# The first stage of a four-layer kernel: input load, group norm, shifted copies and diagonal matrices done in another way

## The chip, the cores and the metric

The kernel runs as one program on one core of a Trainium2 chip. A core has five engines that run at the same time: TensorE (PE in the profile, with PEld its weight loads), VectorE (DVE), ScalarE (ACT), GpSimd (POOL) and SyncE (SP, which here only issues DMAs). The metric is the device time of one execution in microseconds (us). Before the change it is 3016.59 us, the median of three runs (3013.81 to 3019.69).

## The reference, cut to what matters

The input `x` is (8, 128, 16, 16): 8 images, 128 channels, 256 pixels, all float32. Four layers follow each other. Only the first one and the beginning of the second matter here. The first is `x = x + adder(groupnorm(x), W)`, where the "adder convolution" takes the distance of each 3x3 patch from each filter:

```python
def _gn(v, G=32, eps=1e-5):          # 32 groups of 4 channels, for each image
    ...
    return ((g - m) / jnp.sqrt(s + eps)).reshape(v.shape)

def adder2d(x, W, stride, padding):  # W: (128, 128, 3, 3), padding 1
    ...
    out = -jnp.abs(W_col[:, :, None] - X_col[None, :, :]).sum(1)
```

So each of 128 filters needs, for 9 taps, |w - x| for all 128 channels and 2048 pixels, summed over channels and taps. The second layer is a Mamba branch with short depthwise convolutions; the kernel does these on TensorE with diagonal matrices. Layers three and four are attention, experts, a Performer and a spectral filter; the change does not touch them.

## The kernel before, in words

Channels lie on the 128 partitions. `adder_layer` (L303) does the first layer. Its main loop (L406 to L432) goes over 128 filters, four groups of `FG` = 32, and for each over 9 taps. One step makes a tile `d` of 128 x 2048 from a shifted copy of the normalised image and one weight per channel: either `max(x, w)` on VectorE (L421; two taps may be joined in one tile, L417) or `|w - x|` on ScalarE (L423). TensorE then sums `d` over the partitions with four matmuls of 512 pixels (`add`, L380); the stationary matrix has one column of ones, and the four pixel blocks go to four different groups of 32 columns of the array. For a tap done with `max` the identity |w - x| = 2 max(w, x) - w - x is used, so the sums of x and of w over these taps are needed once: `px` (L386 to L390) sums the images over such taps with 24 matmuls, and `wsum` (L391 to L400) sums the weights with 6 small ones. All matmuls go through the helper at L279, so the profile gives them one line and the tile name tells them apart. Each float32 matmul is two records in the trace.

Ahead of the loop stands the part that the change touches. SP issues the load of `x` in four pieces of two images (L323), then that of the filter weights (L326) and of later layers' weights (L256). ACT's queue issues the constants `cst` (L250; 1261 columns, with the group matrix and the identity in them), `vecs` (L251) and `rows` (L252). One reduction (L346) sums each image per channel, a matmul with the group matrix gives the means `mu`, L350 subtracts them, eight ScalarE instructions square and sum (L354), a second matmul gives the variances, L358 and L362 the inverse root, and eight VectorE instructions (L364) write the normalised image into a zero-bordered tile `pad`. GpSimd zeroes `pad` (L342), and makes three copies of it, `sh0` to `sh2`, shifted by 0, 1 and 2 columns (L371). GpSimd also builds 30 diagonal matrices for the second layer (`diagonals`, L473), with the identity times one vector of `vecs` each; in GpSimd's order these 30 stand ahead of the three copies.

The order of the instructions of an engine comes from a scheduler by priority, except in stretches under `manual_schedule`, where program order is kept. The tiles `d` for VectorE and ScalarE have four buffers each. Semaphores of DMAs are handed out round robin from eight: a ninth DMA waits, on the engine that issues it, until the first of the eight has landed. `mamba_layer` (L453) starts with `first_unit` (L670), which multiplies spare matrices on TensorE in its pauses (`meanwhile`, L676).

Of the kernel before, what the change touches and what calls it, by code (L numbers as in the profile page):

```python
# [54 lines left out]
LN_EXP = "natural_log_exp_and_others"  # L55
GELU = "gelu_and_others"
# [28 lines left out]
def _constants():  # L85

    p = np.arange(P)
    c = {}
    c["ident"] = np.eye(P, dtype=np.float32)
    c["group"] = (p[:, None] // 4 == p[None, :] // 4).astype(np.float32) / 1024.0  # L90
# [78 lines left out]
def _weights(x):  # L169
# [3 lines left out]
    w["adder"] = x["L0_conv_W"].reshape(P, P, 9).transpose(1, 2, 0)  # L173
    w["in_proj"] = x["L1_conv_in_proj_w"].T
# [40 lines left out]
class Env:  # L215
# [32 lines left out]
    def load_shared(self):  # L248
        nc = self.nc
        nc.scalar.dma_start(self.cst, self.dram["cst"])  # L250
        nc.scalar.dma_start(self.vecs, self.dram["vecs"])  # L251
        nc.scalar.dma_start(self.rows, self.dram["rows"].partition_broadcast(P))  # L252

    def load_weights(self):
        for k, t in self.w.items():
            self.nc.sync.dma_start(t, self.dram[k])  # L256

# [42 lines left out]
JOINED = (0, 2)  # L300


def adder_layer(E):  # L303
# [8 lines left out]
    with ExitStack() as ctx:  # L312
# [9 lines left out]
        for b in range(0, B, 2):  # L322
            nc.sync.dma_start(x[:, b : b + 2, :], E.dram["x"][b : b + 2].rearrange("b c s -> c b s"))  # L323
        E.load_shared()
        w = p.tile([P, 9, P], F32, tag="w", name="w0")
        nc.sync.dma_start(w, E.dram["adder"])  # L326
        E.load_weights()
# [13 lines left out]
        pad = p.tile([P, B, 18, 18], F32, tag="pad", name="pad0")  # L341
        nc.gpsimd.memset(pad, 0.0)  # L342


        s1 = p.tile([P, B], F32, tag="s1", name="s1")
        nc.vector.tensor_reduce(s1, x, AX.X, ALU.add)  # L346
        mu = ps.tile([P, B], F32, tag="st", name="mu0")
        E.mm(mu, E.c("group"), s1)
        xc = p.tile([P, B, L], F32, tag="xc", name="xc0")
        nc.vector.tensor_tensor(xc, x, bc(mu[:, :], 2, L), ALU.subtract)  # L350
        s2 = p.tile([P, B], F32, tag="s2", name="s2")
        for b in range(B):
            sq = accp.tile([P, L], F32, tag="sq", name="sq0")
            nc.scalar.activation(sq, xc[:, b, :], AF.Square, accum_out=s2[:, b : b + 1])  # L354
        var = ps.tile([P, B], F32, tag="st", name="var0")
        E.mm(var, E.c("group"), s2)
        rs = p.tile([P, B], F32, tag="rs", name="rs0")
        nc.scalar.activation(rs, var, AF.Sqrt, bias=E.eps)  # L358

        nc.scalar.activation(E.sg, E.r("sigma"), AF.Sqrt)  # L360
        nc.scalar.activation(E.sg, E.sg, AF.Sqrt)
        nc.vector.reciprocal(rs, rs)  # L362
        for b in range(B):
            nc.vector.tensor_scalar_mul(  # L364
                pad[:, b, 1:17, 1:17], xc[:, b, :].rearrange("p (h w) -> p h w", w=16), rs[:, b : b + 1]
            )

        shifted = []
        for kw in range(3):
            t = p.tile([P, B, 18 * 16], F32, tag=f"sh{kw}", name=f"sh{kw}")  # L370
            nc.gpsimd.tensor_copy(t.rearrange("p b (h w) -> p b h w", w=16), pad[:, :, :, kw : kw + 16])  # L371
            shifted.append(t)
        nc.gpsimd.tensor_sub(E.center, E.c("ident"), E.mean)
        diagonals(E)

        def tap(k):
            kh, kw = divmod(k, 3)
            return shifted[kw][:, :, kh * 16 : kh * 16 + L]

        def add(out, lhsT, src, start, stop):  # L380

            for i in range(NBLK):
                E.mm(out[i * FG : (i + 1) * FG, :], lhsT, src[:, 2 * i : 2 * i + 2, :], start, stop)


        px = ps.tile([P, BLK], F32, tag="px", name="px0")  # L386
        for k in MAX_TAPS + MORE_TAPS:
            add(px, neg[:, int(k in MORE_TAPS), :], tap(k), k == MAX_TAPS[0], k == MORE_TAPS[-1])
# [1500 lines left out]
```

## Time and profile before

| what | value |
|---|---|
| median of 3 runs | 3016.59 us (3013.81 to 3019.69) |
| the profiled execution: its time | 3019.29 us |
| the profiled execution: its span, first to last instruction | 3017.5 us |
| PE busy over the span | 2848.3 us, 94% |
| DVE busy | 2426.0 us, 80% |
| ACT busy | 2270.8 us, 75% |
| POOL busy | 724.3 us, 24% |
| mean granted TensorE clock | 0.987 |
| first-layer sums `o` on PE: 8512 records | 922.8 us busy |
| `d` on ACT (L423): 472 | 899.6 us busy |
| `d` on DVE (L421): 592, and joined (L417): 88 | 724.3 and 206.7 us busy |

How to read it: the span is counted from the first instruction of the profiled execution, and all places in time below are counted from there. A row of groups gives the line, engine and operation, the tiles with their shapes, the count, then the busy time and the mean of one instruction in ns, then the idle time of the engine just before, and what ended it. In a table of windows each row is a stretch of time with each engine's busy time and instruction count, then the granted clock (PEclk), the share of the DMA engines, and GB/s. Matmuls overlap, so the mean of one (593 ns) is far longer than the spacing of two.

### The profile page before, as it was taken

How to read it: one execution, taken by the hardware profiler on the slowest of the kernel's cores; microseconds unless marked ns; L12 is line 12 of the kernel's file. 1: busy time of each engine (PE TensorE's matmuls, PEld its weight loads, DVE VectorE, ACT ScalarE, POOL GpSimd, SP SyncE). 2: the span in 40 equal slices, each digit the busy share in tenths (PEclk: the TensorE clock that was granted, in tenths of full speed). 3: DMA queues.
4: the chain of work that ended last, by engine and by line, in shares of the span. 5: the costliest groups of instructions: out<-in, count | busy, mean ns of one | idle time of the engine just before them, and what ended most of it. 6: DMA issues, size and time to landing. Idle time of an engine off the chain costs nothing.

```text
span 3017.5 us, 41743 instructions
## 1 busy us (share of the span) xinstructions
PE 2848.3 (94%) x16356; PEld 1263.0 (42%) x16356; DVE 2426.0 (80%) x3387; ACT 2270.8 (75%) x2739; POOL 724.3 (24%) x441
## 2 busy tenths in 40 slices
PE   6999999999999788998898998999999999999999
PEld 2222222222223233443343454455555555654444
DVE  6999999999998899999899648887777777784210
ACT  5999999999997777777777434577778778777332
POOL 4000000000000699998999400000000000000110
PEclk9999999999999999999999999999999999999999
DMA  1000000000000444444444200000000000001100
GB/s 41 1 2 5 2 1 5 1 1 5 1 1 4 170 144 148 139 144 145 129 153 142 91 22 8 14 1 14 14 14 1 14 14 1 14 1 46 49 28 14
DMA packets 39194, 131.49 MB, mean 44 GB/s; under 512 B 7490, under 2 KB 10572, under 8 KB 37588
## 3 DMA queue, kind: packets, MB, share of 16 engines
q1 hardware_dynamic: 38564, 128.02, 12.4%
q8 instruction: 129, 2.11, 0.3%
q10 hardware_dynamic: 432, 0.79, 0.1%
q14 instruction: 69, 0.57, 0.1%
HBM read 125.91 MB, written 1.84 MB: 42 GB/s over the span
## 4 chain that ended last, share of the span: by engine, by line
PE 70%; DVE 15%; ACT 8%; POOL 3%; issue 2%; DMA 0%; DVEq 0%; ACTq 0%; POOLq 0%
PE o L279 30%; PE p L279 10%; PE acc L279 5%; DVE st L878 5%; PE g L279 4%; PE conv L279 3%; PE pc L279 2%; PE var L279 2%; PE pf L279 2%; PE pconv L279 2%; PE pq L279 2%; POOL dbu L783 1%; ACT da L796 1%; PE pn L279 1%; PE pa L279 1%
## 5 line engine op out<-in xcount | busy, mean ns | idle before, releaser
L279 PE MATMUL o<-d,sel 128*32 128x512 f32 x8512 | 922.8, 593 | 7.5 <-DVE d L421 5.5
L423 ACT ACTIVATE d<-sh,w 128x2048 f32<-128x2048 f32 x472 | 899.6, 1994 | 30.7 <-PE o L279 23.2
L421 DVE TENSOR_SCALAR d<-sh,w 128x2048 f32<-128x2048 f32 x592 | 724.3, 1291 | 14.1 <-PE o L279 10.1
L783 POOL TENSOR_TENSOR dbu<-du,bs 128x1024 f32<-128x1024 f32 x191 | 445.8, 2358 | 969.7 <-DVE du L755 964.2
L279 PEld LDWEIGHTS o<-d,sel 128*32 128x32 f32 x8512 | 273.8, 110 | 655.7 <-issue 533.1
L878 DVE TENSOR_TENSOR_SCAN st<-da,dbu 128x512 f32<-128x512 f32 x384 | 446.3, 1207 | 18.0 <-POOL dbu L783 14.0
L279 PE MATMUL acc<-st,cst 128*128 128x512 f32 x768 | 378.6, 625 | 51.1 <-DVE st L889 50.8
L796 ACT ACTIVATE da<-delta,neg_a 128x510 f32<-128x510 f32 x384 | 256.8, 684 | 78.6 <-DVE st L878 73.3
L279 PEld LDWEIGHTS acc<-st,cst 128*128 128x128 f32 x768 | 146.0, 198 | 252.4 <-issue 145.6
L889 DVE TENSOR_TENSOR st<-st,pcs 128x1024 f32<-128x1024 f32 x168 | 205.2, 1222 | 18.2 <-DVE st L878 0.5
L417 DVE SCALAR_TENSOR_TENSOR d<-sh,w,d 128x2048 f32<-128x2048 f32 x88 | 206.7, 2349 | 1.9
L1824 ACT COPY ug<-p 128x512 f32<-128x512 f32 x128 | 75.0, 586 | 136.6 <-PE p L279 136.6
L1365 POOL TENSOR_TENSOR lw<-lw,turn 128x640 f32<-128x640 f32 x8 | 10.0, 1255 | 685.7 <-DVE turn L1364 592.7
L1142 ACT ACT_TABLE_LOAD x134 | 171.9, 1283 | 2.4
L788 ACT COPY pcs<-cs 128x512 f32<-128x512 f32 x168 | 97.8, 582 | 53.6 <-DVE st L889 49.0
L279 PE MATMUL conv<-pad,f 128*128 128x512 f32 x288 | 135.0, 596 | 0.9 <-ACT pad L1040 0.6
L279 PE MATMUL p<-un,lw 128*128 128x512 f32 x256 | 123.6, 605 | 3.8 <-DVE un L1436 2.1
L279 PE MATMUL p<-g,lw 128*128 128x512 f32 x256 | 116.4, 597 | 3.9 <-ACT g L1150 3.9
L279 PE MATMUL p<-T,H 128*128 128x512 f32 x256 | 113.0, 600 | 0.8 <-DVE H L1753 0.8
L279 PE MATMUL g<-ug,me 128*128 128x512 f32 (+1 forms) x320 | 112.0, 509 | 0.0
L1150 ACT ACTIVATE ex<-ex 128x352 f32<-128x352 f32 x128 | 62.4, 494 | 51.5 <-DVE ex L1633 50.3
L279 PE MATMUL pf<-lw,rk 128*128 128x352 f32 x256 | 97.5, 478 | 0.4 <-DVE ek L1583 0.2
(362 smaller groups left out, 3898.1 us busy)
## 6 DMA issues: line engine op xcount, KB each, us to landing
bs<-rows SPq DMA_DIRECT2D x96, 512.0 KB, 3.8
cs<-rows SPq DMA_DIRECT2D x96, 512.0 KB, 4.7
m<-in_Mphi SPq DMA_DIRECT2D x8, 1024.0 KB, 4.8
lw<-in_layers SPq DMA_DIRECT2D x8, 948.0 KB, 4.6
f<-in_fuse SPq DMA_DIRECT2D x2, 1152.0 KB, 7.8
T<-in_T SPq DMA_DIRECT2D x1, 2064.0 KB, 7.6
x<-in_x SPq DMA_DIRECT2D x4, 256.0 KB, 6.9
total<-sums SPq DMA_DIRECT2D x16, 64.0 KB, 2.0
```

Source lines behind the costliest of these rows:

```text
L279: self.nc.tensor.matmul(out, lhsT=lhsT, rhs=rhs, start=start, stop=stop)
L417: nc.vector.scalar_tensor_tensor(d, tap(k), wk, d, ALU.max, ALU.add)
L421: nc.vector.tensor_scalar(d, tap(k), wk, None, ALU.max)
L423: nc.scalar.activation(d, tap(k), AF.Abs, scale=-1.0, bias=wk)
L783: nc.gpsimd.tensor_tensor(dbs[r], got[r // NST]["du"], bc(row("bs", r), 1, 2), ALU.mult)
L788: nc.scalar.copy(pcs[r], row("cs", r))
L796: nc.scalar.activation(das[g % 3][:, :, 1:], d[:, :, 1:], AF.Exp, scale=a)
L878: nc.vector.tensor_tensor_scan(st[:, h, :], da, dbs[r][:, h, :], 0.0, ALU.mult, ALU.add)
L889: nc.vector.tensor_tensor(st, st, bc(pcs[r][:, :], 1, 2), ALU.mult)
L1142: S.tc.keep_in_program_order(S.nc.scalar.preload_act_table_set(name))
L1150: S.nc.scalar.activation(out, src, func, **kw)
L1824: nc.scalar.copy(dst, p4)
```

## The change

It changes only what stands ahead of the loop over filters, the order of the nine taps of the very first filter, and the place of a few small instructions that it delays into the loop.

- Loads: the group matrix becomes the first 128 columns of `cst` (divided by -1024 now, so that means come out negated) and is loaded by itself, first on ACT's queue. The four pieces of `x` alternate between SP's and ACT's queues. The rest of `cst`, `vecs` and `rows` come after `x`.
- Norm: done in four pairs of images. A reduction of a pair on VectorE, a matmul for its mean, a small copy on ScalarE, two squares on ScalarE with the negated mean as bias; then for each pair a reduction of the squares on VectorE, a matmul, a square root on ScalarE; then for each pair a reciprocal and two `tensor_scalar` that write straight into `sh1`. `sh0` and `sh2` are copied from `sh1` by ScalarE (six pairs) and VectorE (two pairs). GpSimd only zeroes borders.
- Diagonal matrices: 1.97 MB (128 x 3840 float32) made by the host, loaded by SP after all other weights. GpSimd's 30 instructions go.
- Spare products: `meanwhile` multiplies a matrix of ones by itself (128 columns) 6 times at the start, and once or twice after each of the eight small matmuls.
- `px`: 24 matmuls as before, over the same six taps in another order, now all ahead of the first `o`, with the six `wsum` products between the first ones. All of this is in a stretch with the order written by hand.
- `xsum`, `wsum_sb`, `wall` and two square roots of `sigma` move into the loop, to filter 1.

In the built program, the instructions of every engine behind the first filter stand in the same order as before. The order ahead of it, as built, has three waits to note: on ACT's queue `vecs` waits until the group matrix has landed and `rows` until the second pair of `x` has (semaphores handed out again), and the load of the square-root table and all of ScalarE's work stand behind these two; on PE `mu` and `var` share two PSUM buffers, so the third `mu` waits until ScalarE has read the first; and all `o` stand behind the last `px`.

```diff
--- before.py
+++ after.py
@@ -53,6 +53,7 @@
 LN_EXP = "natural_log_exp_and_others"
+SQRT = "sqrt_and_others"
 GELU = "gelu_and_others"
@@ -86,8 +87,9 @@
     p = np.arange(P)
     c = {}
+    c["group"] = (p[:, None] // 4 == p[None, :] // 4).astype(np.float32) / -1024.0
     c["ident"] = np.eye(P, dtype=np.float32)
-    c["group"] = (p[:, None] // 4 == p[None, :] // 4).astype(np.float32) / 1024.0
     sel = np.zeros((P, 2, 4, NH), np.float32)
     for n in range(2):
@@ -171,6 +173,13 @@
     x = {k: np.asarray(a) for k, a in x.items()}
     w["x"] = x["x"].reshape(B, P, L)
     w["adder"] = x["L0_conv_W"].reshape(P, P, 9).transpose(1, 2, 0)
+    diag = np.zeros((P, len(BRANCHES), 2, 5, P), np.float32)
+    p = np.arange(P)
+    for i, s in enumerate(BRANCHES):
+        diag[p, i, :, 0:4, p] = x[f"L1_conv_conv_w_{s}"].reshape(2, P, 4).transpose(1, 0, 2)
+        diag[p, i, :, 4, p] = x[f"L1_conv_D_{s}"].reshape(2, P).T
+    w["diag"] = diag
     w["in_proj"] = x["L1_conv_in_proj_w"].T
     w["xproj"] = np.stack([x[f"L1_conv_xproj_w_{s}"].T.reshape(2, P, NPROJ).transpose(1, 0, 2) for s in BRANCHES], 1)
     w["dtproj"] = np.stack([x[f"L1_conv_dtproj_w_{s}"].T for s in BRANCHES], 1)
@@ -247,13 +256,14 @@
     def load_shared(self):
         nc = self.nc
-        nc.scalar.dma_start(self.cst, self.dram["cst"])
+        nc.scalar.dma_start(self.cst[:, P:], self.dram["cst"][:, P:])
         nc.scalar.dma_start(self.vecs, self.dram["vecs"])
         nc.scalar.dma_start(self.rows, self.dram["rows"].partition_broadcast(P))
     def load_weights(self):
         for k, t in self.w.items():
             self.nc.sync.dma_start(t, self.dram[k])
+        self.nc.sync.dma_start(self.diag, self.dram["diag"])
     def c(self, name):
         a, b = self.cols["cst"][name]
@@ -298,6 +308,50 @@
 MORE_TAPS = (7,)
 MORE = tuple(r for r in range(FG) if r % 10 in (0, 3, 6))
 JOINED = (0, 2)
+PX_TAPS = (4, 7, 0, 6, 2, 8)
+FIRST = (4, 7, 1, 0, 6, 3, 2, 8, 5)
+def start(E, pool, psum, x, shifted):
+    nc = E.nc
+    spare = psum.tile([P, P], F32, tag="px", name="spare")
+    def meanwhile(n):
+        for _ in range(n):
+            E.mm(spare, E.ones, E.ones)
+    def small(name):
+        return pool.tile([P, B], F32, tag=name, name=name)
+    s1, neg_mu, s2, rs = (small(n) for n in ("s1", "neg_mu", "s2", "rs"))
+    sq = pool.tile([P, B, L], F32, tag="sq", name="sq0")
+    pairs = [slice(2 * i, 2 * i + 2) for i in range(NBLK)]
+    meanwhile(6)
+    for b in pairs:
+        nc.vector.tensor_reduce(s1[:, b], x[:, b, :], AX.X, ALU.add)
+        mu = psum.tile([P, 2], F32, tag="st", name="mu0")
+        E.mm(mu, E.c("group"), s1[:, b])
+        meanwhile(2 if b is not pairs[-1] else 1)
+        nc.scalar.copy(neg_mu[:, b], mu)
+        for i in range(b.start, b.stop):
+            nc.scalar.activation(sq[:, i, :], x[:, i, :], AF.Square, bias=neg_mu[:, i : i + 1])
+    for b in pairs:
+        nc.vector.tensor_reduce(s2[:, b], sq[:, b, :], AX.X, ALU.add)
+        var = psum.tile([P, 2], F32, tag="st", name="var0")
+        E.mm(var, E.c("group"), s2[:, b])
+        meanwhile(1 if b is not pairs[-1] else 2)
+        nc.scalar.activation(rs[:, b], var, AF.Sqrt, bias=E.eps, scale=-1.0)
+    for b in pairs:
+        nc.vector.reciprocal(rs[:, b], rs[:, b])
+        for i in range(b.start, b.stop):
+            dst = shifted[1][:, i, 1:17, :].rearrange("p h w -> p (h w)")
+            nc.vector.tensor_scalar(dst, x[:, i, :], neg_mu[:, i : i + 1], rs[:, i : i + 1], ALU.add, ALU.mult)
+        nc.scalar.copy(shifted[0][:, b, 1:17, 1:16], shifted[1][:, b, 1:17, 0:15])
+    for i, b in enumerate(pairs):
+        op = nc.vector.tensor_copy if i < 2 else nc.scalar.copy
+        op(shifted[2][:, b, 1:17, 0:15], shifted[1][:, b, 1:17, 1:16])
 def adder_layer(E):
@@ -319,11 +373,13 @@
         ps = ctx.enter_context(tc.tile_pool(name="l0ps", bufs=2, space=PSUM))
         x = last.tile([P, B, L], F32, tag="x", name="x0")
-        for b in range(0, B, 2):
-            nc.sync.dma_start(x[:, b : b + 2, :], E.dram["x"][b : b + 2].rearrange("b c s -> c b s"))
-        E.load_shared()
+        nc.scalar.dma_start(E.cst[:, :P], E.dram["cst"][:, :P])
+        for i in range(NBLK):
+            two = slice(2 * i, 2 * i + 2)
+            (nc.scalar if i % 2 else nc.sync).dma_start(x[:, two, :], E.dram["x"][two].rearrange("b c s -> c b s"))
         w = p.tile([P, 9, P], F32, tag="w", name="w0")
         nc.sync.dma_start(w, E.dram["adder"])
+        E.load_shared()
         E.load_weights()
@@ -338,66 +394,37 @@
         nc.gpsimd.memset(neg[:, 1, :], 0.0)
         for r in MORE:
             nc.gpsimd.memset(neg[:, 1, r : r + 1], -1.0)
-        pad = p.tile([P, B, 18, 18], F32, tag="pad", name="pad0")
-        nc.gpsimd.memset(pad, 0.0)
-        s1 = p.tile([P, B], F32, tag="s1", name="s1")
-        nc.vector.tensor_reduce(s1, x, AX.X, ALU.add)
-        mu = ps.tile([P, B], F32, tag="st", name="mu0")
-        E.mm(mu, E.c("group"), s1)
-        xc = p.tile([P, B, L], F32, tag="xc", name="xc0")
-        nc.vector.tensor_tensor(xc, x, bc(mu[:, :], 2, L), ALU.subtract)
-        s2 = p.tile([P, B], F32, tag="s2", name="s2")
-        for b in range(B):
-            sq = accp.tile([P, L], F32, tag="sq", name="sq0")
-            nc.scalar.activation(sq, xc[:, b, :], AF.Square, accum_out=s2[:, b : b + 1])
-        var = ps.tile([P, B], F32, tag="st", name="var0")
-        E.mm(var, E.c("group"), s2)
-        rs = p.tile([P, B], F32, tag="rs", name="rs0")
-        nc.scalar.activation(rs, var, AF.Sqrt, bias=E.eps)
-        nc.scalar.activation(E.sg, E.r("sigma"), AF.Sqrt)
-        nc.scalar.activation(E.sg, E.sg, AF.Sqrt)
-        nc.vector.reciprocal(rs, rs)
-        for b in range(B):
-            nc.vector.tensor_scalar_mul(
-                pad[:, b, 1:17, 1:17], xc[:, b, :].rearrange("p (h w) -> p h w", w=16), rs[:, b : b + 1]
-            )
-        shifted = []
-        for kw in range(3):
-            t = p.tile([P, B, 18 * 16], F32, tag=f"sh{kw}", name=f"sh{kw}")
-            nc.gpsimd.tensor_copy(t.rearrange("p b (h w) -> p b h w", w=16), pad[:, :, :, kw : kw + 16])
-            shifted.append(t)
+        shifted = [p.tile([P, B, 18, 16], F32, tag=f"sh{kw}", name=f"sh{kw}") for kw in range(3)]
+        for t in shifted:
+            for h in (0, 17):
+                nc.gpsimd.memset(t[:, :, h : h + 1, :], 0.0)
+        nc.gpsimd.memset(shifted[0][:, :, 1:17, 0:1], 0.0)
+        nc.gpsimd.memset(shifted[2][:, :, 1:17, 15:16], 0.0)
         nc.gpsimd.tensor_sub(E.center, E.c("ident"), E.mean)
-        diagonals(E)
         def tap(k):
             kh, kw = divmod(k, 3)
-            return shifted[kw][:, :, kh * 16 : kh * 16 + L]
-        def add(out, lhsT, src, start, stop):
-            for i in range(NBLK):
+            return shifted[kw].rearrange("p b h w -> p b (h w)")[:, :, kh * 16 : kh * 16 + L]
+        def add(out, lhsT, src, start, stop, blocks=range(NBLK)):
+            for i in blocks:
                 E.mm(out[i * FG : (i + 1) * FG, :], lhsT, src[:, 2 * i : 2 * i + 2, :], start, stop)
         px = ps.tile([P, BLK], F32, tag="px", name="px0")
-        for k in MAX_TAPS + MORE_TAPS:
-            add(px, neg[:, int(k in MORE_TAPS), :], tap(k), k == MAX_TAPS[0], k == MORE_TAPS[-1])
         xsum = p.tile([P, BLK], F32, tag="xsum", name="xsum")
-        nc.scalar.copy(xsum, px)
-        wsum = []
-        for taps in (MAX_TAPS, MORE_TAPS):
-            pw = ps.tile([P, 1], F32, tag="st", name="wsum")
-            for k in taps:
-                E.mm(pw, w[:, k, :], E.ones[:, 0:1], start=k == taps[0], stop=k == taps[-1])
-            sb = p.tile([P, 1], F32, tag=f"wsum{len(wsum)}", name="wsum_sb")
-            nc.scalar.copy(sb, pw)
-            wsum.append(sb)
-        wall = p.tile([P, 1], F32, tag="wall", name="wall")
-        nc.vector.scalar_tensor_tensor(wall, wsum[1], E.c("more"), wsum[0], ALU.mult, ALU.add)
+        with tc.manual_schedule(engines={nc.tensor.engine, nc.vector.engine, nc.scalar.engine}):
+            nc.scalar.preload_act_table_set(SQRT)
+            start(E, p, ps, x, shifted)
+            wsum = [ps.tile([P, 1], F32, tag="st", name="wsum") for _ in range(2)]
+            weights = [(pw, taps, k) for pw, taps in zip(wsum, (MAX_TAPS, MORE_TAPS)) for k in taps]
+            for n, k in enumerate(PX_TAPS):
+                for i in range(NBLK):
+                    add(px, neg[:, int(k in MORE_TAPS), :], tap(k), n == 0, n == len(PX_TAPS) - 1, (i,))
+                    for pw, taps, t in weights[2 * i : 2 * i + 2] if n == 0 else ():
+                        E.mm(pw, w[:, t, :], E.ones[:, 0:1], start=t == taps[0], stop=t == taps[-1])
@@ -410,6 +437,8 @@
                 maxima = MAX_TAPS + (MORE_TAPS if r in MORE else ())
                 joined = () if r in MORE else JOINED
                 order = (1, 0, 3, 2, 5, 4, 6, 7, 8) if joined else range(9)
+                if g == r == 0:
+                    order = FIRST
                 for k in order:
                     wk = w[:, k, f : f + 1]
                     if k in joined[1:]:
@@ -427,6 +456,17 @@
                     sel = sel2 if k in maxima else sel1
                     row = sel[:, FG - 1 - r : 2 * FG - 1 - r]
                     add(out, row, d, r == 0 and k == order[0], r == FG - 1 and k == order[-1])
+                if g == 0 and r == 1:
+                    pinned = tc.keep_in_program_order
+                    pinned(nc.scalar.copy(xsum, px))
+                    sb = p.tile([P, 2], F32, tag="wsum", name="wsum_sb")
+                    for i in range(2):
+                        pinned(nc.scalar.copy(sb[:, i : i + 1], wsum[i]))
+                    wall = p.tile([P, 1], F32, tag="wall", name="wall")
+                    pinned(nc.vector.scalar_tensor_tensor(wall, sb[:, 1:2], E.c("more"), sb[:, 0:1], ALU.mult, ALU.add))
+                    for src in (E.r("sigma"), E.sg):
+                        pinned(nc.scalar.activation(E.sg, src, AF.Sqrt))
             nc.vector.tensor_add(sums[:, g, :], xsum, out)
             for i in range(NBLK):
                 nc.sync.dma_start(total[g * FG : (g + 1) * FG, i, :], sums[i * FG : (i + 1) * FG, g, :])
@@ -468,15 +508,6 @@
         for p in (F.gated(last), F.convolutions(last)):
             for _ in p:
                 pass
-def diagonals(E):
-    for k, s in enumerate(BRANCHES):
-        for h in range(2):
-            for j in range(4):
-                E.nc.gpsimd.tensor_scalar_mul(E.diag[:, k, h, j, :], E.c("ident"), E.v("cw" + s, 4 * h + j))
-            E.nc.gpsimd.tensor_scalar_mul(E.diag[:, k, h, 4, :], E.c("ident"), E.v("D" + s, h))
 class _Chain:
```

## Prediction

> **What bounds the kernel now.** I read the chain that ended last for its first 60 us, then windows over the first layer, then the timeline and groups of the beginning. The chain:
>
> ```profile
> 1.19 5.31 DMA vecs<-in_vecs
> 6.49 0.09 issue
> 6.58 2.34 POOL diag L478 x4
> ...
> 24.61 2.06 POOL sh L371
> 26.67 0.02 issue
> 26.69 7.39 DVE d L421
> 34.08 0.04 issue
> 34.13 1.06 PE o L279
> ...
> 36.04 5.43 PE px L279 x36
> 41.47 0.04 PE o L279 x3
> ```
>
> To 24.6 us GpSimd's diagonal matrices hold up its copies `sh`. The first `d` then takes 7.39 us, where its group takes 1.29: GpSimd copies and zeroes until 32.99. From 34.13 PE is on the chain and stays. By 41.47 it has done 40 `px` records and 4 of `o`; the other 8508 `o` records end at 963.92, so 922.45/8508 = 0.1084 us each. Undisturbed, `o` would have begun at 41.47 - 4 x 0.1084 = **41.0 us**. Is PE alone the limit after that?
>
> ```profile
> 34.00:42.00 8.00, 7.87 (x52) 2.19 (x56) 3.65 (x4) 2.43 (x3) 0.00 (x0) 1.00 0.00 0
> 42.00:963.00 921.00, 918.96 (x8500) 273.11 (x8496) 911.32 (x679) 894.25 (x473) 0.00 (x0) 1.00 0.01 2
> ```
>
> PE is busy 99.8%, DVE 98.9%, ACT 97.1%. PE leads, but DVE has only 9.7 us to spare. Every us by which `px` ends earlier is then a us off the kernel: behind the first filter all engines keep their order, and nothing there waits for anything that this change makes later. So the sum is one date: when `o` can begin in the changed kernel.
>
> **Loads.** The first engine rows are:
>
> ```profile
> 9.51 2.29 DVE L346 TENSOR_REDUCE s<-x 128x8 f32<-128x2048 f32 x1 [9.51 <-DMA x<-in_x]
> 12.48 2.29 DVE L350 TENSOR_TENSOR xc<-x,mu 128x2048 f32<-128x2048 f32 x1 [0.69 <-PE mu L279]
> 19.15 0.20 DVE L362 RECIPROCAL rs<-rs 128x8 f32<-128x8 f32 x1 [4.38 <-ACT rs L358]
> 19.46 2.95 DVE L364 TENSOR_SCALAR pad<-xc,rs 128x256 f32<-128x256 f32 x8
> ```
>
> `x` lands 5.3 to 7.1 us after issue, with 630 KB of constants moving beside it. Bytes moved, summed over half-microsecond windows: 0.15 MB by 3.0 us, 0.67 by 4.5, 0.85 by 5.0, 1.66 by 8.0. The skill's first page (Trainium Kernel Development and Optimization, Key Constraints) says that all issuing engines share the same 16 DMA engines, so that issuing from several saves issue time only. By that rule splitting `x` over two queues gives at most the 1.5 us between the first and last issue (0.7 and 2.2). I follow it: the split itself gives nothing more, the new order does. The second pair is in when group matrix, two pairs and perhaps 0.2 MB of the third have moved, 0.77 MB: about 4.8, plus 0.9 until it counts as landed (0.85 MB had moved at 5.0, the 0.63 MB of constants and their share of `x`; the constants landed at 5.7): 5.7 us. Ends: 5.0 (no competition) and 7.9 (the median of before).
>
> This pair matters more than the first: `rows` waits for it on ACT's queue, and the table load and all of ScalarE's norm stand behind. Issue of `rows` 0.45, table load 1.28. For a table switch the skill (ScalarE: Activation LUTs, What ACT_TABLE_LOAD costs) gives about 2.66 us with a drain. The trace differs:
>
> ```profile
> 2320.14 1.28 ACT L1142 ACT_TABLE_LOAD   x1
> 2321.43 1.27 ACT L1150 ACTIVATE g<-p,vecs 128x512 f32<-128x512 f32 x2
> ```
>
> The next activation starts 1.29 after the load. The rule would put all that follows 1.4 later; I take the row. ScalarE starts at 5.7 + 0.5 + 1.3 = **7.5**.
>
> **Norm.** Per pair a copy (0.16 as L397, 0.03 to the next) and two squares 0.40 apart (L354): 1.0; four pairs end at **11.6**. The last pair of `x` competes with the 0.58 MB of filter weights behind the others: 1.7 MB, at 8.0 or 8.9; reduction a quarter of 2.29 plus start, 0.69, and the mean 0.6: 10.2, just under the 10.5 at which ScalarE reaches it. Covered, with 0.3 to spare; an `x` 1 us later costs 0.7. Then VectorE reduces the last squares (0.69 and handovers): 12.4. Per pair now a reciprocal with handover 0.31 (19.15 to 19.46) and two `tensor_scalar`. L364 has one scalar operand, 0.37 apart; L702, two operands on 512 columns, 0.55. For 256 columns 0.37 spacing, 0.42 for the last: 1.1 a pair, four end `sh1` at **16.7**; ends 15.6 (0.3 apart) and 17.8.
>
> **Copies.** ScalarE ends the last `sh0` 0.6 later (480 columns, like the 586 ns of a 512 copy), its two `sh2` at 18.5. VectorE's two cost 0.35 to 0.65 each, so its first `d` runs 17.9 to 19.2 and its second to 20.4. GpSimd's borders and zeroing (about 4 us, L342 and L923 as rows) are over before. None of this is last: `px` is.
>
> **TensorE.** The first `px` block can start with the first pair of `sh1`, 12.4 + 1.1 = 13.5. A block alone uses a quarter of the columns, so its two records cost what full-width ones do: 0.43 each (four blocks share 8 x 0.108 = 0.87 us). After each of three blocks four `wsum` records follow that need all columns: 0.22 apart in the trace (2.7 us for 12), which was cold; I take 0.15, ends 0 and 0.22. So 0.87 + 0.6 = 1.47 per pair against VectorE's 1.1: the fourth block starts at 13.5 + 3 x 1.47 = **17.9**, not at 16.7. Its column group still has six taps to do in order, 6 x 0.87 = 5.2: `px` ends and `o` begins at **23.1**. `sh0` (17.3) and `sh2` (18.5) are in time for taps three and five; `d` (19.2, 20.4) for `o`. Were `px` free, `d` would be next late, at 19.2.
>
> **Spare products.** In the old beginning PE ran `px` at half speed: from 34.14 four records took 0.85, until about 38.9, then 0.43. TensorE: Matmul & The Clock Gate (Part 1) says why: cold until busy for a window of about 3.4 us. The rule speaks against the six first products: 12 records, 0.126 each warm (18 in 2.27 us), 0.25 cold, are 3 us, less than a window. But behind them PE has a mean, spares or a variance in nearly each us from 5 to 13, and in the trace a window only 48% busy (966 to 969.4) kept the full clock. Whether such a window also wins it, nothing shows. I take warm; cold costs at most 3 x 1.2 more in the first blocks and ends as PE gets busy, so 2 to 3 us. The spares delay no one: each is 0.25 warm behind a 1.0 us beat.
>
> **Removed and moved at no cost.** GpSimd's 30 matrices and 3 copies (18.3 and 6.2 us) were on the path and are counted in the old 41.0. The 1.97 MB of diagonals take about 5.5 us at 360 GB/s behind SP's other weights, ending near 17; needed at 983, and SP's next issue is near 275. `xsum` (0.59), `wsum_sb` (0.32) and the roots (0.43) go into ACT's 27 us of slack.
>
> **Sum.** 41.0 - 23.1 = 17.9 us. On the profiled execution, 3019.3 - 17.9 = 3001.4. That execution is 2.7 above the median of the runs, so by the median 3016.6 - 17.9 = **2998.7**.
>
> **Rivals.**
> A, the sum: gain 15.8 to 20.2 with the ends above, 60%.
> B, PE is cold for `px`: the fourth block starts near 20 to 21, `o` at 25.5: gain 15.5, 3001.1. For it: the first spares are too short. Against: the later ones. 15%.
> C, the beginning is quicker: second pair at 5.0, `wsum` hidden, VectorE 0.8 a pair: `sh1` at 14.8, `o` at 20.0: gain 21, 2995.6. 15%.
> D, the change doesn't load `x` earlier: second pair at 7.9, all 2.2 later, gain 15.7, 3000.9. For it: the last pieces moved at only 120 to 260 GB/s from 6.0 to 7.5. 7%.
> E, slower: VectorE becomes the bound of the first layer. 680 instructions share 9.7 us of slack, 14 ns each; from 41 ns (3%) more on each, as other places of `sh` in memory might give, the gain is gone, and at 60 ns the layer loses 31 - 18 = 13 us: 3030. Against: shapes, strides and order are the same, GpSimd is idle there in both. 2%.
> Within 0.2% (6 us, about what a measurement of this kernel can tell): only mixtures of D and E, 1%.
> The range is A to D with 2 us for the spread of medians (single runs went from -2.8 to +3.1): 2993 to 3003.5. Faster 0.97, same 0.01, slower 0.02.
>
> **What would show it.** In the changed profile: ScalarE's first copy near 7.5, just behind a table load that waited for `rows`; `sh1` done near 16.7; the fourth `px` block near 17.9, waiting for `wsum` and not for `sh1`; `px` records in fours 0.43 apart (0.85: B); first `o` near 23; PE busy from there on, `o` ending near 946 instead of 963.9. Wrong would be: an idle PE between the first `o` and 100 us (then `d` was late), DVE means over 1.31 us (E), or a second layer longer than before.

## The result and the profile after

The changed kernel takes 3007.27 us, the median of 12 runs (2999.28 to 3010.62), against 3016.04 us for 12 runs of the kernel before beside them: the ratio of the means (3005.85 and 3016.07) is 0.9966 with a 95% interval of 0.9956 to 0.9976. So it is faster, by 8.8 us in the medians and 10.2 in the means and not by 17.9, and the time lies outside the predicted range. All runs of these kernels, those of the experiments below among them (25 of the changed kernel, 82 of the one before) have means of 3005.2 and 3015.6 us: a gain of 10.4 us, with a standard error of 0.8 (10.2, 10.3 and 13.2 in the three batches that hold both kernels).

The profiled execution of the changed kernel took 3000.94 us (span 2999.2). Beside the profile of before (3019.29) that would be a gain of 18.3 us, as predicted. Both profiles lie at an edge of their spread, one at the slow end, one at the fast end; what that hides is the subject of most of what follows. The chain that ended last, for its first 60 us:

```profile
1.18 3.95 DMA x<-in_x
...
5.14 0.33 ACTq L261
...
6.80 0.17 ACT neg_mu L337
...
14.89 1.85 PE px L289 x2
16.74 0.82 PE wsum L289 x4
17.56 0.98 PE px L289 x2
...
20.58 4.84 PE px L289 x41
...
25.85 34.16 PE o L289 x318
```

GpSimd has left the chain. PE holds it from 9.88 us without a pause: means, spares, variances, then `px`. I call it a turn when one block of `px` (two images, two records, a quarter of the columns) is followed by its four `wsum` records; there are three turns, then comes the fourth block with the remaining taps of all four. The first turn takes 2.67 us (14.89 to 17.56), the second 1.51. The profile's record of the granted clock has full speed from 17.28 us. The rows of ScalarE and of VectorE around it:

```profile
5.51 1.28 ACT L418 ACT_TABLE_LOAD   x1 [5.51 <-DMA x<-in_x]
6.80 0.16 ACT L337 COPY neg_mu<-mu 128x2 f32<-128x2 f32 x1
...
10.46 0.16 ACT L337 COPY neg_mu<-mu 128x2 f32<-128x2 f32 x1 [0.59 <-PE mu L289]
```

```profile
9.03 0.69 DVE L333 TENSOR_REDUCE s<-x 128x2 f32<-128x512 f32 x1 [2.60 <-DMA x<-in_x]
...
14.92 0.73 DVE L350 TENSOR_SCALAR sh<-x,neg_mu,rs 128x256 f32<-128x256 f32 x2
```

The table load starts when `rows` has been issued, which waited for the second pair of `x`; the first copy follows 1.29 us after the start of the load, as the row of before said. `sh1` is complete at 15.65. The first `o` starts at 24.83. Behind it the layer is bound as before; engines in the columns PE, PEld, DVE, ACT, POOL, then the granted clock:

```profile
42.00:943.00 901.00, 898.94 (x8310) 271.63 (x8309) 893.98 (x668) 880.35 (x464) 0.00 (x0) 1.00 0.01 2
```

PE is busy 99.8% again, with 2.06 us idle where it had 2.04. The last `o` ends at 948.43 instead of 963.86: 15.4 us earlier. The rest of the program takes 2050.73 us instead of 2053.63, so 2.9 of the 18.3 us come from code that the change does not touch. The chain at the end of the layer, before and then after:

```profile
937.04 26.86 PE o L279 x248
963.92 0.70 DVE sums L430
```

```profile
921.61 26.86 PE o L289 x248
948.50 0.70 DVE sums L470
```

### The profile page after: what moved, and what is told of

It is laid out like the page before. It is cut to its first block, busy times and chain, and to the rows that moved or that the text cites. A ratio compares the mean times of both kernels' runs of the same rounds, so it can differ in the third digit from the quotient of the medians.

```text
span 2999.2 us, 41845 instructions
## 1 busy us (share of the span) xinstructions
PE 2854.1 (95%) x16404; PEld 1275.4 (43%) x16404; DVE 2419.8 (81%) x3398; ACT 2273.2 (76%) x2744; POOL 699.6 (23%) x415
## 4 chain that ended last, share of the span: by engine, by line
PE 70%; DVE 16%; ACT 7%; POOL 3%; issue 3%; DMA 1%; DVEq 0%; ACTq 0%; POOLq 0%
PE o L289 30%; PE p L289 10%; DVE st L909 5%; PE acc L289 5%; PE g L289 4%; PE conv L289 3%; PE pc L289 2%; PE var L289 2%; PE pf L289 2%; POOL dbu L814 2%; PE pq L289 2%; PE pconv L289 1%; PE pn L289 1%; PE pa L289 1%; ACT da L827 1%
## 5 line engine op out<-in xcount | busy, mean ns | idle before, releaser
L450 DVE TENSOR_SCALAR d<-sh,w 128x2048 f32<-128x2048 f32 x592 | 718.4, 1281 | 11.0 <-PE o L289 10.9
L909 DVE TENSOR_TENSOR_SCAN st<-da,dbu 128x512 f32<-128x512 f32 x384 | 446.2, 1206 | 17.9 <-POOL dbu L814 13.8
```

The costliest lines, as they stand in the source:

```text
L450: nc.vector.tensor_scalar(d, tap(k), wk, None, ALU.max)
L909: nc.vector.tensor_tensor_scan(st[:, h, :], da, dbs[r][:, h, :], 0.0, ALU.mult, ALU.add)
```

## The experiments

Three explanations were open: PE's clock is low for `px`, and the gain is smaller by that much in most executions; the spare products delay what they should serve; and later layers give part of the gain back (the third theory in the expectations). For each profile I compare three numbers: the first `o`, the end of the last `o`, and the rest, which is the span less that end. Each ratio is to runs of the kernel before from the same batch (runs made together); their medians are 3016.04 for after, 3015.64 for after_again, before_again, no_spares and host_diag, 3016.73 for hot and the three last_first kernels, and 3018.55 for after_third, bare_again and consts_on_sp.

| kernel | first `o` | last `o` ends | rest | median (runs) | ratio to before, 95% |
|---|---|---|---|---|---|
| before | 34.13 | 963.86 | 2053.63 | 3016.04 (12) | |
| before_again | 33.68 | 962.92 | 2046.70 | 3014.54 (13) | 0.9986 to 1.0005 |
| after | 24.83 | 948.43 | 2050.73 | 3007.27 (12) | 0.9956 to 0.9976 |
| after_again | 29.16 | 952.70 | 2050.17 | 3004.65 (7) | 0.9955 to 0.9980 |
| after_third | 25.50 | 949.08 | 2054.71 | 3005.66 (6) | 0.9942 to 0.9969 |
| no_spares | 28.50 | 952.02 | 2046.71 | 3003.41 (6) | 0.9951 to 0.9975 |
| host_diag | 28.75 | 958.72 | 2051.83 | 3010.43 (21) | 0.9973 to 0.9986 |
| hot | 21.69 | 945.28 | 2053.84 | 3001.46 (6) | 0.9941 to 0.9973 |
| last_first | 25.75 | 948.57 | 2050.72 | 3000.60 (6) | 0.9937 to 0.9964 |
| last_first_hot | 24.44 | 947.23 | 2052.94 | 3001.38 (6) | 0.9928 to 0.9964 |
| last_first_bare | 22.23 | 945.06 | 2052.18 | 2999.10 (6) | 0.9933 to 0.9960 |
| bare_again | 23.67 | 946.44 | 2050.79 | 2999.43 (5) | 0.9928 to 0.9951 |
| consts_on_sp | 22.48 | 945.25 | 2046.55 | 2996.36 (6) | 0.9921 to 0.9946 |

In the kernel before and in host_diag some `px` records stand behind the first `o`, so there only the end of the last `o` is to be compared.

**Both kernels once more, unaltered.** No edit.

> The changed kernel once more, for its spread. The profiled executions differ by 18.3 us (3017.5 to 2999.2), but the medians by 9. Theory 1 (the clock): the first layer always ends 15 to 16 us earlier than before (near 948.5), and what follows takes 2047 to 2061 us, by where the 3.41 us windows of the TensorE clock happen to fall; times of single executions then go with 1 - clock (3000 us at 0.989, 3008 at 0.984), and the medians of many executions differ by about 15. Theory 2 (an unsteady beginning): the first layer ends anywhere from 948 to 957, by when x lands and when the clock comes up, and what follows takes the same as in the first profile (2050.7); single times don't go with the clock. Theory 3 (given back later): in most executions what follows takes 6 to 8 us more than it does in executions of the kernel before, with the first layer at 948.5.

> The kernel before once more, for the clock and the length of its single executions. Theory 1: 3012 to 3020 with a clock from 0.990 down to 0.984, the first layer ending at 963.9 within 1 us in any profile, the rest 2047 to 2056. Theory 2: first layer 963.9, rest 2053.6 and little spread with the clock. Theory 3: the rest is 2047 to 2054, shorter than the changed kernel's in executions of its slower kind.

The changed kernel's second profile loses 4.3 us of the gain, all of it before the first `o`. PE's timeline of after_again (start, duration of the group, tiles, count):

```profile
13.68 1.92 PE L289 MATMUL px<-sh,neg 128*32 128x512 f32 x2
15.53 1.01 PE L289 MATMUL wsum<-ones,w 128*128 128x1 f32 x4
16.47 1.91 PE L289 MATMUL px<-sh,neg 128*32 128x512 f32 x2
...
22.04 5.35 PE L289 MATMUL px<-sh,neg 128*32 128x512 f32 x24
```

`px` begins 1.1 us earlier than in the first profile, yet each turn takes 2.79 us (13.68 to 16.47) where it takes 1.51 at full clock, and the fourth block starts at 22.04. The record has full clock only from 27.70 us. Before_again ends its first layer within 1 us of the first profile of before. Its rest, however, is 6.9 us shorter with not one instruction changed: one profile of each kernel can't measure a change of 9 us. Of the three theories none holds alone: the layer's end varies, as the second says (948.43 and 952.70), but single times also go with the granted clock of the whole execution, as the first says. Of the changed kernel's 25 runs, the 12 with a clock of 0.987 or less take 3008.3 us on average, the other 13 take 3002.3 (correlation -0.72; -0.82 in 70 runs of before whose clocks are on record). That clock is a mean over the execution and doesn't say in which layer it was low.

**The spares left out.**

```diff
     def meanwhile(n):
-        for _ in range(n):
-            E.mm(spare, E.ones, E.ones)
+        pass
```

> The changed kernel without any spare product at its start. If the spares bring the clock up for px (they did by 17.2 us in the first profile): px and its wsum run at half rate until PE has been busy for one to two windows, 18 to 22 us, so that the first layer ends 1 to 3 us later than with them (949.5 to 951.5). If they do nothing: the same 948.5, or a few tenths earlier, as no mean or variance stands behind them. Theory 1 on what follows: unchanged spread. Theory 2: much less or much more spread than with the spares.

```profile
9.76 0.56 PE L289 MATMUL mu<-s,cst 128*128 128x2 f32 x2 [2.00 <-DVE s L332]
10.35 1.15 PE L289 MATMUL var<-s,cst 128*128 128x2 f32 x4
11.66 1.22 PE L289 MATMUL var<-s,cst 128*128 128x2 f32 x4 [0.15 <-ACT rs L344]
...
13.16 1.89 PE L289 MATMUL px<-sh,neg 128*32 128x512 f32 x2 [0.28 <-DVE rs L346]
```

From the last mean to the first `px` are 3.4 us (9.76 to 13.16). With spares at half clock they are 5.0 (9.86 to 14.82 in the first profile of after), 4.9 (8.78 to 13.68 in after_again) and 5.0 (10.64 to 15.61 in after_third): on TensorE each variance stands behind two spare records, and `px` behind all of them. VectorE isn't held up: its first reciprocal comes 2.33 us after the last mean in no_spares and in the first profile of after (9.76 to 12.09, 9.86 to 12.19). Without spares `px` is at half clock until 26.94. The layer ends at 952.02, half a microsecond outside what was expected: near after_again (952.70), where `px` ran just as slowly, and 3 to 3.6 us later than in the two profiles where the clock came up during `px`. By time the kernels with and without spares can't be told apart (means 3003.9 and, over all runs of the changed kernel, 3005.2, with standard errors of 1.3 and 0.7). The spares as built bought nothing that these runs can measure.

**Only the diagonal matrices.** The kernel before, with the 30 matrices from the host and nothing else of the change.

```diff
+        self.nc.sync.dma_start(self.diag, self.dram["diag"])
...
-        diagonals(E)
```

> The kernel before with one part of the change alone: the diagonal matrices come from the host. By the profile of before, the copies sh can start when pad is ready (22.4) and not behind the last matrix (24.56), and all that follows keeps its distances: first layer earlier by 2.1 us, 3014 by the median. If the matrices on GpSimd had also slowed VectorE's norm[...], up to 1 us more. Theory 1 for the rest: as before.

The layer gains more than expected. It ends 5.1 us earlier than in the first profile of before, 4.2 earlier than in the second, and the median is 5.2 lower than that of before in the same runs. VectorE's and GpSimd's rows say how:

```profile
25.60 3.10 DVE L427 TENSOR_SCALAR d<-sh,w 128x2048 f32<-128x2048 f32 x1 [2.16 <-POOL sh L378]
```

```profile
23.46 7.20 POOL L378 COPY sh<-pad 128x2304 f32<-128x2304 f32 x3 [17.57 <-DVE wall L406]
```

The copies `sh` now start as soon as `pad` is made and `wall` is done, although `x` came later here (VectorE's reduction starts at 11.16 against 9.51). VectorE's first `d` beside GpSimd's copies takes 3.10 us instead of 7.38 (why it differs so much, no run shows), and the eight `pad` instructions, with GpSimd idle, 2.19 instead of 2.95. By the chains PE has done all of `px` by 35.9, where it was 41.9.

**Denser spares.**

```diff
-    meanwhile(6)
+    meanwhile(8)
...
-        meanwhile(2 if b is not pairs[-1] else 1)
+        meanwhile((4, 4, 2, 2)[b.start // 2])
...
-        meanwhile(1 if b is not pairs[-1] else 2)
+        meanwhile(2)
```

> The changed kernel with more spare products: 8 at the start, 4, 4, 2, 2 behind the means and 2 behind each variance (6; 2, 2, 2, 1; 1, 1, 1, 2 in the change). Theory: what the prediction missed is px at half clock. In two profiles of three with the new beginning the clock came up only at 27 to 28 us, after px[...]. These fill over 80% from 1 to 9 us: full clock from about 8 us, a pair of px and wsum in 1.5 us instead of 2.8, first o at 23 to 24.5, first layer done at 946.5 to 948 in the profile, median near 3000.5 and a spread that only the later layers make. Rival (the loss is elsewhere, later or in the landing of x): first layer at 950 to 953 and a median of 3004 to 3006, as without.

```profile
12.83 1.05 PE L289 MATMUL px<-sh,neg 128*32 128x512 f32 x2
...
14.34 1.04 PE L289 MATMUL px<-sh,neg 128*32 128x512 f32 x2
...
17.37 4.91 PE L289 MATMUL px<-sh,neg 128*32 128x512 f32 x41
21.69 0.60 PE L289 MATMUL o<-d,sel 128*32 128x512 f32 x3
```

Full clock from 7.10 us; every turn takes 1.51 us, the fourth block starts at 17.37 and the first `o` at 21.69, 7.5 us earlier than in after_again and earlier than expected (23 to 24.5). That is the predicted sum's arithmetic, come true once the clock does what the prediction took for granted: with the spacing of the turns it shows the cause of the missing part of the first layer. The layer ends at 945.28, where 946.0 was predicted. By time the denser spares gain nothing certain: the mean is 3002.6 (standard error 1.5), single times still go from 2998.21 to 3008.85, and whether the clock comes up early in every execution one profile doesn't show.

**The last block first.** With the fourth block's first product ahead, PE waits until all of `sh1` is there and then does all four blocks at once; `wsum` goes into the wait.

```diff
+            for pw, taps, t in weights:
+                E.mm(pw, w[:, t, :], E.ones[:, 0:1], start=t == taps[0], stop=t == taps[-1])
             for n, k in enumerate(PX_TAPS):
-                for i in range(NBLK):
+                for i in (3, 0, 1, 2):
                     add(px, neg[:, int(k in MORE_TAPS), :], tap(k), n == 0, n == len(PX_TAPS) - 1, (i,))
-                    for pw, taps, t in weights[2 * i : 2 * i + 2] if n == 0 else ():
-                        E.mm(pw, w[:, t, :], E.ones[:, 0:1], start=t == taps[0], stop=t == taps[-1])
```

> The changed kernel, with px starting with the last pair of images and wsum in the wait ahead of it. Theory: the first three px blocks, alone on a quarter of the columns, gain nothing (the fourth column group still has six taps to do) and hold up the fourth behind three turns of wsum: 17.9 in the sum, 20.6 and 22.0 in the profiles. Then the fourth block starts when its image is ready (15.5 to 16), px fills all columns at once, which also brings the clock up within 3.4 to 6.8 us: first o at 22.5 to 24.5, first layer at 946 to 948, median near 3000. Rival (these turns are covered, only the clock counts): o as late as before, 25 to 29.

The same with the denser spares, and the same with no spares at all:

> Both: dense spares, and px from the last pair on. Theory: full clock when px starts near 15.5 to 16, px in 5.2 us, first o at 21 to 22, first layer at 944.5 to 945.5, median near 2998. If dense spares only delay the variances and the clock falls again before px (its windows from 10 to 14 us are half full at best): o near 24, first layer at 947.

> The same and no spare products at all. In the profile without spares the way from the last mean to the first px block took 3.4 us, with them 4.9: at half clock each variance waits behind two spare records. Theory: 1 to 1.5 us earlier than with spares, first o at 21.5 to 23.5, first layer 945 to 947. Rival (the spares do bring the clock up in time): the same or up to 2 us later.

PE's timelines, last_first_hot and then last_first_bare:

```profile
14.31 2.56 PE L289 MATMUL wsum<-ones,w 128*128 128x1 f32 x12
16.80 7.82 PE L289 MATMUL px<-sh,neg 128*32 128x512 f32 x48
24.44 1.03 PE L289 MATMUL o<-d,sel 128*32 128x512 f32 x8
```

```profile
12.53 2.70 PE L289 MATMUL wsum<-ones,w 128*128 128x1 f32 x12
15.49 6.93 PE L289 MATMUL px<-sh,neg 128*32 128x512 f32 x48 [0.27 <-DVE sh L349]
22.23 3.19 PE L289 MATMUL o<-d,sel 128*32 128x512 f32 x28
```

In last_first, with the changed kernel's spares, `px` begins at 17.81 and runs at half clock until 23.42; its first `o`, 25.75, misses the 22.5 to 24.5 expected. Last_first_hot misses its 21 to 22 too, and the other course that its expectation named came instead: the clock rose at 4.74, fell to half again at 11.6 and returned at 21.8; the `wsum` products, queued behind spares at half clock, held `px` until 16.80. Without spares (last_first_bare, which differs from last_first in nothing else and has its first `o` 3.5 us earlier) PE does `wsum` in a pause, waits 0.27 us for `sh1`, and 48 records of `px` take 6.7 us, of which the first half is at half clock. The last block can't start before `sh1` is complete in any of these versions, and turns that use a quarter of the columns only stand in its way: in hot, with every turn at full clock, the fourth block still starts 2.2 us after `sh1` is complete (15.20, 17.37). By time last_first and last_first_bare (means 3000.7 and 2999.5, standard errors 0.4 and 0.7) are clearly below the changed kernel's 3005.2; the last_first kernels and hot can't be told from each other (3002.6 for hot, 2999.8 for last_first_hot, standard errors 1.5 and 1.7), so whether a warm start beats a cold one in this order stays open.

**A third sample, and the issue of `rows` moved.** After_third and bare_again are unaltered copies of the changed kernel and of last_first_bare. Consts_on_sp is last_first_bare with three issues on another queue:

```diff
-        nc.scalar.dma_start(self.cst[:, P:], self.dram["cst"][:, P:])
-        nc.scalar.dma_start(self.vecs, self.dram["vecs"])
-        nc.scalar.dma_start(self.rows, self.dram["rows"].partition_broadcast(P))
+        nc.sync.dma_start(self.cst[:, P:], self.dram["cst"][:, P:])
+        nc.sync.dma_start(self.vecs, self.dram["vecs"])
+        nc.sync.dma_start(self.rows, self.dram["rows"].partition_broadcast(P))
```

> The changed kernel unaltered, a third sample. Theory (its place depends on whether the clock comes up before px): either the full clock comes up by 18 us, px turns 1.5 us, o at 24.3 to 25.3 and the first layer ends at 948 to 949; or it stays half until 26 to 28 us, turns 2.8 us, o at 28.5 to 29.5, end at 952 to 953. Rival (a fixed cost elsewhere): an end between the two, or outside both, with no connection to the clock. Median, from 19 earlier runs (mean 3005.4): 3003 to 3008.

> The kernel with the last block first and no spare products, unaltered, as the partner of the next one and as a second sample. If its order of blocks makes it independent of the clock: o at 22 to 22.5 and the first layer's end at 945 to 945.5 again, median 2998.5 to 3001. If its first profile was luck: o near 25, end near 948.

> As the partner, with the rest of cst, vecs and rows issued from SP's queue behind the filter weights instead of ACT's. Tests the step that ScalarE starts only when the second pair of x has landed, because rows waits for it on ACT's queue. If that step is right: the table load runs before 4 us, ScalarE's first copy follows the first mean near 5.0 instead of 7.2, the squares of the first three pairs end before the last pair of x has its mean (near 9.5), and the squares end about 10.6 instead of 11.2; o and the first layer's end come 0.4 to 0.7 us earlier than the partner's (near 21.6 and 944.5). If the last pair of x lands later behind more bytes on SP's side: no gain or a loss of up to 0.5 us. If ScalarE waits for x and not for rows: the first copy stays near 7.2.

After_third shows a third course of the clock: full from 4.17 to 7.6 us, half to 17.8, then full. Its PE timeline, and a window with the granted clock behind POOL's column:

```profile
15.61 1.92 PE L289 MATMUL px<-sh,neg 128*32 128x512 f32 x2
17.45 0.77 PE L289 MATMUL wsum<-ones,w 128*128 128x1 f32 x4
18.15 1.04 PE L289 MATMUL px<-sh,neg 128*32 128x512 f32 x2
```

```profile
14.00:15.00 1.00, 1.00 (x6) 1.00 (x6) 0.95 (x4) 0.41 (x3) 0.00 (x0) 0.50 0.38 92
```

PE is busy all of that microsecond and still at 0.50. One turn is cold (at half clock), the others are not; the first `o` comes at 25.50, slightly after the window that the expectation gave (24.3 to 25.3 beside an end of 948 to 949; the end is 949.08), since `px` also began 0.8 us later than in the first profile. Bare_again missed its expectation: 23.67 instead of 22 to 22.5, because full clock came at 21.41 and not at 18.71. So that order is not independent of the clock, only less exposed to it: 1.4 us between two profiles, against 4.3 us among three of the changed kernel. Single times of the two runs of this version lie between 2997.85 and 3002.68, those of the changed kernel between 2999.14 and 3010.62.

Consts_on_sp answers the question whether `rows` on ACT's queue holds ScalarE back. ScalarE's timeline, bare_again and then consts_on_sp:

```profile
5.68 1.28 ACT L417 ACT_TABLE_LOAD   x1 [5.68 <-DMA x<-in_x]
6.98 0.16 ACT L336 COPY neg_mu<-mu 128x2 f32<-128x2 f32 x1
```

```profile
2.18 1.28 ACT L417 ACT_TABLE_LOAD   x1 [2.18 <-issue]
5.35 0.16 ACT L336 COPY neg_mu<-mu 128x2 f32<-128x2 f32 x1 [1.89 <-PE mu L289]
```

With nothing on ACT's queue that waits, the table is loaded at 2.18 and the first copy starts at 5.35, where bare_again has 6.98: the prediction's reading, that `rows` holds ScalarE back, is right. The first `o` and the end of the layer come 1.2 us earlier than bare_again's, more than the 0.4 to 0.7 expected. The last pair of `x` was reduced from 7.81 there and from 8.91 in bare_again (8.42 in last_first_bare); whether the other order of the loads did that, or chance, two profiles can't say; last_first_bare, the same kernel as bare_again, was as early as consts_on_sp (22.23 and 945.06), so a gain in time isn't shown. The median of 2996.36 us is the lowest of all kernels here, 9.3 below the changed kernel's among the same runs.

## Why the prediction was wrong

**The bound, and what lies behind the first filter: right.** PE limits the layer in every version; 923.6 us lie between the first and the last `o` in all three profiles of the changed kernel, 922.9 were expected. Rival E, a VectorE that becomes the bound, did not come: it is idle for 7.0 of the 901 us in the window above, where it was 9.7 of 921, and the median of L421, now L450, is 1281 ns in both. The stretch is 0.7 us longer than expected because the prediction let `o` begin when `px` ends; the first `o` starts 1.0 us before the last `px` record has ended (24.83 and 25.85 in the first profile). Counted from that end the stretch is 922.6, as it is in last_first_bare (22.42 to 945.06).

**Loads and norm: right, and pessimistic in parts.** ScalarE began at 6.79 to 6.92 us in the three profiles (7.5 predicted), `sh1` was done at 15.65, 15.1 and 16.4 (16.7): VectorE takes 0.85 us a pair, not 1.1. The row that the 1.1 was taken from, 2.95 us for eight instructions, had GpSimd busy beside it; with GpSimd idle host_diag has 2.19. Of the loads only the last pair's date, `x` reduced from 9.03 in the first profile, cost something: ScalarE waited 0.59 us for its mean. What splitting `x` over two queues does by itself, no run here shows.

**TensorE: the step that failed.** The prediction said "I take warm; cold costs at most 3 x 1.2 more in the first blocks and ends as PE gets busy, so 2 to 3 us", and "The spares delay no one". Both are wrong. In none of the three profiles was the first turn warm, and in one no turn was:

| | predicted | after | after_again | after_third |
|---|---|---|---|---|
| `sh1` complete | 16.7 | 15.65 | 15.1 | 16.4 |
| first `px` | 13.5 | 14.82 | 13.68 | 15.61 |
| fourth block starts | 17.9 | 20.51 | 22.04 | 21.17 |
| from there to the first `o` | 5.2 | 4.3 | 7.1 | 4.3 |
| from there to the end of `px` | 5.2 | 5.3 | 8.1 | 5.3 |
| first `o` | 23.1 | 24.83 | 29.16 | 25.50 |
| full clock from | the first `px` on | 17.28 | 27.70 | 4.2 to 7.6, then 17.82 |

At half clock the three turns cost 8.4 us where 4.4 were counted, and the records behind them, which the prediction had at full speed in each case, 2 to 3 us more; spares ahead of each variance delay the first `px` by 1.5. Rival B had the mechanism and its date (25.5), and two of three profiles are near it; its chance of 15% was too low, and after_again (29.16) shows that it had too small a price. The Trainium skill (TensorE: Matmul & The Clock Gate, Part 1) says that one busy window of about 3.4 us is needed; the length agrees with the steps of 3.41 us in these records, but in the first profile of after a step in which the profile shows PE busy throughout (10.45 to 13.87) left the clock at half. The prediction saw that the first six products fall short of it and set against this that a window only 48% busy had kept the full clock. What keeps the clock doesn't win it: that step and the two ahead of it, 74% and 79% busy by the same measure, didn't. The denser spares of hot, which differ in nothing else, bear this out.

**The sum.** Over the profiles the first layer ends at 950.1 us on average (three) instead of 963.4 (two): 13.3 us. The 4.6 us missing from 17.9 are 3.4 for the later `o`, 0.7 for the stretch behind it and 0.5 because the profiled execution of before was itself a little late in this layer. The timed runs show 10.4, standard error 0.8. The last 2.9 us are not settled. They are less than twice their own error (1.6, the three layer ends alone scatter by 4.3), and in the same five profiles the whole program gains 11.6, since the rest is 1.7 longer in the three than in the two. With all turns cold in more of the timed executions than in one of three they would be explained too, since after_again's layer gains only 10.7; a timed run shows no `px`, so that stays a guess. Part of the first result's distance is the sample: the gain is 8.8 by the medians of those 12 runs each and 10.2 by their means, and the three runs of before that the prediction started from had a median 1.0 above the mean of 82.

**That later layers give the gain back: not seen.** Over the ten profiles with the new beginning the rest has a mean of 2050.9 us, over the three with the old 2050.7. But it goes from 2046.6 to 2054.7 among all thirteen, so a loss of 2 us could hide in it. It grows by about 0.3 us for each microsecond that the granted clock is at half behind the first layer (58.0 to 77.1 us; correlation 0.76). The first pair of profiles seemed to confirm the prediction by luck: 2.9 us of its 18.3 came from this rest, and its first layer gained 2.1 more than the average.

## What to carry to other kernels

Work that TensorE does right after a quiet beginning is to be costed at half clock unless the trace of that very stretch shows the full one, and spares meant to raise it must fill PE densely; the sparse ones here delayed the chain instead. When several blocks end together, let the one whose input comes last go first rather than use the pauses of its predecessors: with the same spares that took the mean from 3005.2 to 3000.7. Twelve runs of each kernel gave a difference of 10 us in 3000 only to within 3, and a profile is to be read stage by stage, since the stages that a change doesn't touch move by as much as the change.

## What was not expected of the hardware

- Within each profile all changes of the clock lie on one grid of about 3.41 us, and the phase of these steps (the place of the grid in time) differed between executions of one kernel; so the same instructions got full clock at 17.28, 27.70 and 17.82 us.
- What raises it isn't fully settled. I estimate the share of such a step in which products stream (a record over 512 pixels takes 0.43 us at full clock and twice that at half, one over 128 a quarter of it), weighted by the share of the array's columns they use. So counted, the spares of the changed kernel mostly gave 0.43 to 0.75, and the clock rose once, after 0.75; 0.74 and 0.69 left it at half. After 0.80 and 0.94 (hot, last_first_hot) it rose, and it fell again after 0.32 (after_third) and 0.35 (last_first_hot). Two steps of 0.17 with lone `px` blocks, a quarter of the columns, left it at half in after_again; but it rose after 0.33 in the first profile and after 0.38 in after_third, where spares were followed by a lone block. Without the weights these two steps are 0.70 and 0.75, but 0.74 in after_again and 0.71 in hot left it at half, and in hot it stayed at full after a weighted 0.13 (0.50 without). No rule of mine covers all of these.
- The granted clock in a table of windows reads 1.00 where no change has been recorded yet: between 15 and 27 us in after_again, while `px` came at half pace. The spacing of equal instructions is the better witness there. The last of these windows:

```profile
25.00:27.00 2.00, 2.00 (x12) 0.39 (x8) 0.00 (x0) 0.00 (x0) 0.00 (x0) 1.00 0.00 0
```

- One instruction of VectorE took 7.38 us in the profile of before and 3.10 in host_diag where 1.28 is usual, beside GpSimd's copies in both.
